# Attention's k: turned by VectorE in 32x32 squares and by DMAs through device memory, and the output product cut in two halves

## Chip, cores and metric

The kernel runs on one core of a Trainium2 chip, in fp32 throughout. The metric is the device time of one execution in microseconds (us), taken as the median of several runs. The engines are named as in the profile: PE is TensorE (PEld its weight loads), DVE is VectorE, ACT is ScalarE, POOL is GpSimd, SP is SyncE, which here only issues DMAs.

## The reference

The input x is 2 x 2048 x 256. Four residual blocks follow each other, each on a layer norm of x: a gated linear scan, a feed-forward layer with ternary weights, a higher-order linear attention (`hla`), and the same feed-forward layer again. The change lies in the attention:

```python
q = (x @ W_q).reshape(b, t, H, DK).transpose(1, 0, 2, 3)   # H = 16 heads, DK = DV = 64
k = (x @ W_k).reshape(b, t, H, DK).transpose(1, 0, 2, 3)
v = (x @ W_v).reshape(b, t, H, DV).transpose(1, 0, 2, 3)
def step(carry, qkv):
    S_K, C_QV, G = carry
    q_t, k_t, v_t = qkv
    k_C = einsum('bhk,bhkv->bhv', k_t, C_QV)
    G = G + k_t[..., :, None] * k_C[..., None, :]
    S_K = S_K + k_t[..., :, None] * k_t[..., None, :]
    C_QV = C_QV + q_t[..., :, None] * v_t[..., None, :]
    S_C = einsum('bhkj,bhjv->bhkv', S_K, C_QV)
    o_t = einsum('bhk,bhkv->bhv', q_t, S_C - G)
    return ((S_K, C_QV, G), o_t)
_, outs = scan(step, zeros, (q, k, v))
return outs.reshape(b, t, H * DV) @ W_o
```

## The kernel before

Three stages stand in program order: `front` (scan and first feed-forward layer), `attention`, and the second feed-forward layer. Within a stage PE, DVE, ACT and POOL run their instructions in the order in which the code issues them (`manual_schedule`); each engine works through its own queue in order and waits by semaphores for what it reads and for the buffers that it overwrites.

The attention works in 32 steps s (`NS`), one for each chunk of 128 tokens of each of the 2 sequences: step s is sequence s % 2, chunk n = s // 2. Even steps are called `first` in the code. The 1024 features of 16 heads are 8 pairs (`NPR`) of two heads, 128 features each; a chunk is processed as two halves of 64 tokens (`CH`). The projections q, k and v of two chunks, one for each sequence, are made together by seven products instead of eight (class `Seven`, its method `go`). They are spread over the steps: k of the next pair of steps is made in an even step, q and v in an odd one. `kN` holds k with tokens on the partitions. The operands q and k of the first product have to lie with features on the partitions (`qT`, `kT`); `qT` is made so at once, `kT` is turned from `kN`.

A step issues, in this order:

- `inter(s, "S", "uT")` (L838): q times the running sum S of k k^T, into `huT`;
- `products(s, "kT", "p1")` (L819): 64 small products of q and k into the two banks `hp`; DVE multiplies them by a causal mask into `p1` (L826);
- `outward(s - 2)` (L893): the output product of step s-2, 8 products of 128x256 into `hy`, which the trace shows as 16 matmuls; DVE adds `hy` to x (L898);
- `intra(s, "S", ..., "p1", "uT")` (L852) and `intra(s - 1, "M", ..., "p2", "oT")`: the masked part of this step and, one step late, of the second product; ACT and DVE copy the banks to `uT` and `oT`;
- parts of the projections, and between them `units(s)`: 8 transposes of u (`huN`, L805) which DVE copies to `uN` (L806);
- `update` (L874): S for step s+1 and M for step s, whose chunk sums DVE adds (L884);
- more of the projections, then `inter(s, "M", "oT")` and `products(s, "uT", "p2")` with its masks;
- the last product of k (even steps) or q (odd steps) and, in odd steps, the transposes of the next normalised x (`pt`, L199, copied by ACT, L202);
- `keys(s + 1)`: 8 transposes of k for the next step (`hkT`, L805) into two banks, which DVE copies to `kT` (L806).

In the last two steps parts of the first block of the next stage (`last.fill`) take the place of the projections. Before the loop, `keys(0)` and the projections of the first pair fill a start-up part. Each buffer named here is single (`bufs=1`), except `qT`, `kN`, `vN` and the sums with three. The PSUM has 8 banks in three rings: four "ps" (used by `hp`, `hy`, `hkT`, `huN`, `hS`, `hM`, `pt` and one bank of each projection), two "uT" and two "oT"; `bank` takes the next of its ring. The DMAs of the loads are issued at the start by SP and ACT; in the attention no DMA is issued before the output stores of its end.

In `front`, `ternary_sum` adds up the sizes of w1 on DVE (L225), `ternary_total` adds the 8 partial sums (L236), and `ternary_scale` sums over partitions by a product `pm` on PE (L242).

Of the kernel before, what the change touches and what calls it, by code (L numbers as in the profile page):

```python
# [17 lines left out]
FP = mybir.dt.float32  # L18
AF = mybir.ActivationFunctionType
ALU = mybir.AluOpType  # L20
AX = mybir.AxisListType

P = 128
B, T, D = 2, 2048, 256
# [4 lines left out]
NPR = H * DK // P  # L29
NCH = B * T // P  # L30
CPB = T // P
BC = 4
BT = BC * P
NBLK = T // BT
CH = 64
HF, HB, HD, HK = NF // 2, BT // 2, D // 2, H * DK // 2
LN_EPS = 1e-5
RMS_EPS = 1e-12
# [3 lines left out]
def kernel(  # L42
# [15 lines left out]
    nc = tc.nc  # L58
# [7 lines left out]
    def bank(shape, name, tag="ps"):  # L66

        ring = rings[tag]
        ring.append(ring.pop(0))
        return psum_pool.tile(shape, FP, tag=f"bank{ring[-1]}", bufs=1, name=name)  # L70
# [6 lines left out]
    x_sb = const.tile([P, NCH, D], FP, name="x_sb")  # L77
# [156 lines left out]
    def ternary_total(pool, part, name):  # L234
        tot = pool.tile([P, 1], FP, tag="tot", name=f"tot_{name}")
        nc.vector.tensor_reduce(tot, part, AX.X, ALU.add)  # L236
        return tot

    def ternary_scale(pool, w, tot, name):
        n = w.shape[1] * w.shape[2]  # L240
        pm = bank([P, 1], f"pm_{name}")
        nc.tensor.matmul(pm, lhsT=ones, rhs=tot, start=True, stop=True)  # L242
        hs = pool.tile([P, 1], FP, tag="hs", name=f"hs_{name}")
        nc.vector.tensor_scalar(hs, pm, 1.0 / (P * n), 1e-8, ALU.mult, ALU.max)
        nc.vector.tensor_scalar_mul(hs, hs, 0.5)
        nhs = pool.tile([P, 1], FP, tag="nhs", name=f"nhs_{name}")
        nc.vector.tensor_scalar_mul(nhs, hs, -1.0)
        return hs, nhs
# [281 lines left out]
    def front(scan_pool, ffn_pool, tern_pool, then, later):  # L530
        last = [{} for _ in range(B)]
# [35 lines left out]
        scales = {}  # L567

        def quarters_1():
            scales[1] = ternary_scale(tern_pool, w1, ternary_total(tern_pool, sum1, "w1"), "w1")  # L570
            tern(w1, scales[1], 0)
            tern(w1, scales[1], 1)

# [10 lines left out]
        s_(2)  # L584
        t_(1)
        q_(0, 1)
        sum1 = ternary_sum(tern_pool, w1, "w1", True)
        r_(2)
        q_(1, 0)
        s_(3)  # L590
# [99 lines left out]

    def attention(keep, pool, state, last):
        halves = [slice(0, CH), slice(CH, P)]

        def feats(h, p):
# [114 lines left out]
        def products(s, left, nm):  # L811


            b, n = steps[s]
            banks = [bank([P, NPR, CH], f"h{nm}{b}_{n}_{h}") for h in range(2)]
            for p in range(NPR):
                for c in range(2):
                    for h in range(2):
                        nc.tensor.matmul(  # L819
                            banks[h][halves[c], p, :], lhsT=d[s][left][halves[h], p, halves[c]],  # L820
                            rhs=d[s]["qT"][halves[h], p, halves[c]], start=True, stop=True,
                        )
            d[s][nm] = []
            for h in range(2):
                pm = pool.tile([P, NPR, CH], FP, tag=f"{nm}{h}", bufs=1, name=f"{nm}{b}_{n}_{h}")
                nc.vector.tensor_tensor(pm, banks[h], mask8, ALU.mult)  # L826
                d[s][nm].append(pm)

        def inter(s, sums, nm):

# [14 lines left out]
        def intra(s, sums, nat, pm, nm, evict):  # L845

            b, n = steps[s]
            banks = d[s][nm + "b"]
            for p in range(NPR):
                for c in range(2):  # L850
                    for h in range(2):
                        nc.tensor.matmul(  # L852
                            banks[c][halves[h ^ c], p, :], lhsT=d[s][nat][halves[c], feats(h, p)],
                            rhs=d[s][pm][h][halves[c], p, :],
                            start=(d[s][sums][c] is None and p == 0), stop=True,
                            skip_group_check=True,
                        )
            t = pool.tile([P, NPR, P], FP, tag=nm, bufs=1, name=f"{nm}{b}_{n}")
            evict(t[:, :, halves[0]], banks[0])  # L859
            for h in range(2):  # L860
                evict(t[halves[h], :, halves[1]], banks[1][halves[h ^ 1], :, :])
            d[s][nm] = t
# [23 lines left out]
                prev = t  # L886
            before[b, sums] = prev

        def outward(s):
            b, n = steps[s]  # L890
            py = bank([P, D], f"hy{b}_{n}")
            for p in range(NPR):
                nc.tensor.matmul(  # L893
                    py, lhsT=d[s]["oT"][:, p, :], rhs=wo[:, p, :],
                    start=(p == 0), stop=(p == NPR - 1),
                )
            xs = x_sb[:, b * CPB + n, :]
            nc.vector.tensor_tensor(xs, xs, py, ALU.add)  # L898

        def keys(s):  # L900
            kN = d[s]["kN"]
            turned(lambda p: kN[:, p * P : (p + 1) * P], s, "kT")

        def units(s):
            uT = d[s]["uT"]
# [12 lines left out]
        k.go(0, 5, 6)  # L918
        q.go(0, 5, 6)
        xn = norm_rows(norm_pool, pair(1), stats)  # L920
        k.go(7)
        q.go(7)
        k.go(3)
        q.go(3)
        k.go(4)
        q.go(4)
        v = Seven(0, "vN", "oT")
        v.go(2, 1)
        keys(0)
        v.go(0, 5, 6)  # L930
        update(0, "kN", "kN", "S")
        v.go(7, 3)
        for s in range(NS):
            first, n = s % 2 == 0, s // 2
            more = n + 1 < CPB
            inter(s, "S", "uT")
            products(s, "kT", "p1")
            if first and n + 2 < CPB:
                stats = norm_stats(norm_pool, pair(n + 2), bias=True)
            elif s == NS - 4:  # L940
                last.stats()
            elif s == NS - 2:
                last.second_stats()
            if s == 0:
                v.go(4)
                pairs[1] = norm_turned(norm_pool, pair(1), xn, bufs=1)
                pair_sums(1)
            if s % 2 == 1 and more:
                q, v = Seven(n + 1, "qT", "uT"), Seven(n + 1, "vN", "oT")
            if s == 1:  # L950
                q.go(2)
                v.go(2)
            if s >= 2:
                outward(s - 2)
                d[s - 2].clear()
            intra(s, "S", "kN", "p1", "uT", act)
            if s > 0:
                intra(s - 1, "M", "vN", "p2", "oT", dve)
            if not more:
                last.begin(first)  # L960
                fill = last.fill
                fill(2)
                units(s)
                fill(2)
            elif first:
                k = Seven(n + 1, "kN", "uT")
                k.go(2, 1)
                units(s)
                k.go(0, 5, 6)
            else:  # L970
                if s > 1:
                    q.go(2)
                    v.go(2)
                q.go(1)
                units(s)
                v.go(1)
                q.go(0, 5)
                v.go(0, 5)
                q.go(6)
                v.go(6)  # L980
            if first and n + 2 < CPB:
                xn = norm_rows(norm_pool, pair(n + 2), stats)
            elif s == NS - 4:
                last.rows()
            elif s == NS - 1:
                last.second_rows()
            if s + 1 < NS:
                update(s + 1, "kN", "kN", "S")
            update(s, "uN", "vN", "M")
            if not more:  # L990
                fill(2)
            elif first:
                k.go(7, 3)
            else:
                v.go(7)
                q.go(7)
                v.go(3, 4)
                q.go(3)
            inter(s, "M", "oT")
            products(s, "uT", "p2")  # L1000
            if not more:
                fill(1)
            elif first:
                k.go(4)
            else:
                q.go(4)
            if not first and n + 2 < CPB:
                pairs[n + 2] = norm_turned(norm_pool, pair(n + 2), xn, bufs=1)
                pair_sums(n + 2)
            elif s == NS - 3:  # L1010
                last.turned()
            if s + 1 < NS:
                keys(s + 1)
        last.out()
        outward(NS - 2)
        intra(NS - 1, "M", "vN", "p2", "oT", act)
        last.out()
        outward(NS - 1)

    pairs = {}  # L1020

# [83 lines left out]
    with tc.tile_pool(name="keep", bufs=3) as keep_pool:  # L1105
        with (
            tc.tile_pool(name="attn", bufs=1) as attn_pool,
            tc.tile_pool(name="state", bufs=1) as state_pool,
            tc.manual_schedule(engines=by_hand),
        ):  # L1110
            last = Last(keep_pool, attn_pool)
            attention(keep_pool, attn_pool, state_pool, last)

# [62 lines left out]
```

## Time and profile before

| | us |
|---|---|
| median of 3 runs (1275.59 to 1276.32) | 1275.65 |
| the profiled execution, its own time | 1276.43 |
| its span, from the first to the last instruction | 1274.2 |
| the attention's loop, from the first `hp` to the last transposes of k, about | 332 to 1054 |
| PE busy in 332 to 1054 (722.00) | 720.84 |
| DVE busy there | 418.61 |
| ACT busy there | 188.95 |

An even step in the middle took 20.2 us (560.28 to 580.49), an odd one some 24.6. The granted clock of PE is 1.00 throughout. The page puts the instructions in groups: line, engine, operation, output and inputs, shapes, count, then the busy time in us and the mean of one in ns, and behind a second bar how long the engine stood idle just before them and what ended that. The "chain that ended last" follows the program back from its end: at each piece to what released it, or to the piece before it on the same engine; in it pieces don't overlap, so its pieces can be added up, while the durations of the groups contain the latency of overlapping matmuls.

### The profile page before, as it was taken

What the parts mean: (1) busy time and instruction counts of PE and PEld (TensorE: products, weight loads), DVE (VectorE), ACT (ScalarE), POOL (GpSimd) and SP (SyncE); (2) the same over time, 40 slices, a digit from 0 to 9 for tenths busy, and PEclk for the clock granted to TensorE, in tenths of its full rate; (3) what the DMA queues carried; (4) which work ended last, traced back from release to release, by engine and by line L of the source; (5) the groups of instructions that cost most, each with busy time, mean ns of one, the idle gap of its engine ahead of it and who ended that gap; (6) DMA issues with size and microseconds to landing.
All of it is one profiled execution on the core that took longest, in us unless ns stands there. A gap on an engine that the chain in (4) does not pass through costs nothing.

```text
span 1274.2 us, 46893 instructions
## 1 busy us (share of the span) xinstructions
PE 1266.2 (99%) x21748; PEld 1031.6 (81%) x21748; DVE 748.7 (59%) x1375; ACT 435.3 (34%) x846; POOL 244.9 (19%) x427
## 2 busy tenths in 40 slices
PE   9999999999999999999999999999999999999998
PEld 6578877998677877877777778778778788999998
DVE  7965664655555555555555565565555665556654
ACT  4345554444322132222232222222222323444542
POOL 3742233331110110110110110110110120232221
PEclk9999999999999999999999999999999999999999
DMA  9100000000000000000000000000000000010000
GB/s 325 35 1 1 1 1 1 1 1 1 3 3 3 4 3 3 4 3 3 4 3 3 4 3 3 3 3 3 4 3 3 4 3 3 17 34 17 18 18 33
DMA packets 13042, 18.59 MB, mean 15 GB/s; under 512 B 784, under 2 KB 11792, under 8 KB 12848
## 3 DMA queue, kind: packets, MB, share of 16 engines
q1 hardware_dynamic: 12336, 15.21, 3.5%
q8 instruction: 170, 2.79, 0.9%
q0 software_dynamic: 80, 0.14, 0.1%
q10 hardware_dynamic: 432, 0.26, 0.1%
q14 instruction: 24, 0.20, 0.1%
HBM read 11.41 MB, written 4.19 MB: 12 GB/s over the span
## 4 chain that ended last, share of the span: by engine, by line
PE 98%; DMA 1%; DVE 1%; ACT 0%; issue 0%; POOL 0%; DVEq 0%; POOLq 0%
PE hy L893 9%; PE ox L473 9%; PE hx L382 9%; PE pq L269 6%; PE hkN_X L765 5%; PE hp L819 5%; PE hqT_X L760 5%; PE hvN_X L765 5%; PE oz L473 4%; PE hz L382 4%; PE huT L852 3%; PE hS L874 3%; PE huT L838 3%; PE hoT L838 3%; PE hM L874 2%; PE hoT L852 2%
## 5 line engine op out<-in xcount | busy, mean ns | idle before, releaser
L826 DVE TENSOR_TENSOR p<-hp,mask 128x512 f32<-128x512 f32 x128 | 82.4, 686 | 75.5 <-PE hp L819 75.5
L718 POOL TENSOR_TENSOR S<-xnT 128x128 f32<-128x128 f32 x32 | 14.6, 457 | 577.4 <-ACT xnT L202 559.7
L893 PE MATMUL hy<-wo,oT 128*128 128x256 f32 x512 | 119.2, 385 | 0.0
L893 PEld LDWEIGHTS hy<-wo,oT 128*128 128x128 f32 x512 | 94.6, 190 | 14.1 <-issue 0.5
L394 ACT ACTIVATE hT<-hT,b_sb 128x256 f32<-128x256 f32 x192 | 85.4, 500 | 33.9 <-DVE hT L426 32.4
L859 ACT COPY uT<-huT 128x512 f32<-128x512 f32 x32 | 18.8, 586 | 220.0 <-PE huT L852 220.0
L269 PE MATMUL pq<-xnT,wqkva 128*128 128x512 f32 (+1 forms) x216 | 85.0, 547 | 0.3 <-ACT xnT L213 0.3
L884 DVE TENSOR_TENSOR S<-S,hS 128x512 f32<-128x512 f32 x60 | 41.2, 687 | 71.7 <-PE hS L874 68.6
L269 PEld LDWEIGHTS pq<-xnT,wqkva 128*128 128x128 f32 x216 | 40.0, 190 | 37.5 <-issue 34.0
L185 ACT ACTIVATE xn<-x_sb,nb,rs 128x256 f32<-128x256 f32 x124 | 64.8, 592 | 16.1 <-POOL nb L171 16.1
L382 PE MATMUL hx<-xT,w 128*128 128x256 f32 x256 | 66.1, 381 | 0.0
L479 DVE TENSOR_TENSOR x_sb<-x_sb,ox 128x256 f32<-128x256 f32 x64 | 26.7, 417 | 63.7 <-PE ox L473 63.7
L806 DVE COPY uN<-huN 128x512 f32<-128x512 f32 x64 | 41.2, 685 | 22.7 <-PE huN L805 22.7
L382 PEld LDWEIGHTS hx<-xT,w 128*128 128x128 f32 x256 | 47.9, 190 | 6.4
L153 DVE BATCH_NORM_STATS2 st<-x_sb 128x6 f32<-128x256 f32 x128 | 51.3, 402 | 2.4 <-DMA x_sb<-in_x_dram 2.4
L359 POOL TENSOR_TENSOR xT<-xnT 128x256 f32<-128x256 f32 x15 | 10.9, 729 | 214.9 <-ACT xnT L215 214.9
L874 PEld LDWEIGHTS hS<-kN 64*64 64x64 f32 x1984 | 32.7, 134 | 23.8 <-DVE kN L770 10.6
L859 DVE COPY oT<-hoT 128x512 f32<-128x512 f32 x31 | 21.4, 691 | 50.7 <-PE hoT L852 50.7
L806 DVE COPY kT<-hkT 128x512 f32<-128x512 f32 x64 | 41.2, 686 | 16.6 <-PE hkT L805 16.6
L400 ACT COPY hT<-hx 128x512 f32<-128x512 f32 x32 | 18.8, 586 | 93.3 <-PE hx L382 93.3
L898 DVE TENSOR_TENSOR x_sb<-x_sb,hy 128x256 f32<-128x256 f32 x32 | 13.5, 421 | 52.8 <-PE hy L893 52.7
L465 DVE TENSOR_TENSOR hS<-hT 128x512 f32<-128x512 f32 x62 | 41.2, 685 | 5.6 <-ACT hT L394 5.6
(213 smaller groups left out, 2910.0 us busy)
## 6 DMA issues: line engine op xcount, KB each, us to landing
out_dram<-x_sb SPq DMA_DIRECT2D x16, 256.0 KB, 2.1
x_sb<-in_x_dram SPq DMA_DIRECT2D x7, 512.0 KB, 8.9
w<-in_w_t_dram SPq DMA_DIRECT2D x2, 512.0 KB, 8.9
w<-in_w_t_dram SPq DMA_DIRECT2D x1, 1024.0 KB, 11.1
wk<-in_w_k_dram SPq DMA_DIRECT2D x1, 1024.0 KB, 11.3
wq<-in_w_q_dram SPq DMA_DIRECT2D x1, 1024.0 KB, 12.2
wv<-in_w_v_dram SPq DMA_DIRECT2D x1, 1024.0 KB, 14.2
wo<-in_w_o_dram SPq DMA_DIRECT2D x1, 1024.0 KB, 15.7
```

The costliest lines, as they stand in the source:

```text
L185: nc.scalar.activation(xn[:, c, :], x_sb[:, g, :], AF.Identity, bias=nb[:, c : c + 1], scale=rs[:, c : c + 1],)
L269: nc.tensor.matmul(pq[:, :nt], lhsT=wqkva[:, d, col : col + P], rhs=xnT[:, d, :], start=(d == 0), stop=(d == ND - 1),)
L382: nc.tensor.matmul(at[a][:, j, :], lhsT=A[:, f * P : (f + 1) * P], rhs=Bm, start=(new and j == 0), stop=True, skip_group_check=True,)
L394: nc.scalar.activation(out, out if src is None else src[:, j, :], AF.Gelu, bias=b1_sb[:, f : f + 1])
L473: nc.tensor.matmul(banks[name][:, c, :], lhsT=A[f // 2][:, f % 2, c * P : (c + 1) * P], rhs=Bm[:, f, :], start=(new and c == 0 and f == 0) ...
L760: nc.tensor.matmul(to[:, j, :], lhsT=self.A[i][:, j * P : (j + 1) * P], rhs=self.B[i], start=(new and j == 0), stop=True, skip_group_check ...
L765: nc.tensor.matmul(to, lhsT=self.A[i], rhs=self.B[i], start=new, stop=True, skip_group_check=True)
L806: nc.vector.tensor_copy(t[:, 4 * g : 4 * g + 4, :], pt)
L826: nc.vector.tensor_tensor(pm, banks[h], mask8, ALU.mult)
L838: nc.tensor.matmul(banks[c][halves[h ^ c], p, :], lhsT=d[s][sums][c][halves[h], p, :], rhs=d[s]["qT"][halves[h], p, halves[c]], start=(p = ...
L874: nc.tensor.matmul(banks[c][halves[h], p, :], lhsT=d[s][left][halves[c], feats(h, p)], rhs=d[s][right][halves[c], feats(h, p)], start=True ...
L893: nc.tensor.matmul(py, lhsT=d[s]["oT"][:, p, :], rhs=wo[:, p, :], start=(p == 0), stop=(p == NPR - 1),)
```

## The change

`keys` no longer uses PE. Two steps ahead, at the end of step s, `keys_out(s + 2)` lets DVE turn the 32x32 squares of `kN` into `kS` (in the buffer of `uN`), and SP writes `kS` to device memory as `kD` (512 KB, three such buffers). In step s+1, after `intra`, `keys_in(s + 2)` (called there as `keys_in(s + 1)`) lets SP read `kD` by four DMAs, 32 partitions each, into `kR` (in the buffer of `p1`), where all features of a pair stand on the partitions but the pairs lie interleaved. Later in that step `keys` lets ACT copy `kR`, read at a step of 8 elements, into a contiguous `kT`. The output product is cut in two: `outward(s - 1, 0)`, its first four pairs, stands at the end of step s, `outward(s - 2, 1)`, the last four with the addition to x, in the old place. The masked products `p1` and `p2` become one tile each instead of two. At the start, product 7 and 3 of k are followed at once by `keys_out(0)` and `keys_in(0)`. In `front` the total of w1 is taken right behind its sum.

```diff
-            scales[1] = ternary_scale(tern_pool, w1, ternary_total(tern_pool, sum1, "w1"), "w1")
+            scales[1] = ternary_scale(tern_pool, w1, tot1, "w1")
...
-        sum1 = ternary_sum(tern_pool, w1, "w1", True)
+        tot1 = ternary_total(tern_pool, ternary_sum(tern_pool, w1, "w1", True), "w1")
...
-            d[s][nm] = []
+            d[s][nm] = pool.tile([P, 2, NPR, CH], FP, tag=nm, bufs=1, name=f"{nm}{b}_{n}")
             for h in range(2):
-                pm = pool.tile([P, NPR, CH], FP, tag=f"{nm}{h}", bufs=1, name=f"{nm}{b}_{n}_{h}")
-                nc.vector.tensor_tensor(pm, banks[h], mask8, ALU.mult)
-                d[s][nm].append(pm)
+                nc.vector.tensor_tensor(d[s][nm][:, h], banks[h], mask8, ALU.mult)
...
-        def outward(s):
+        def outward(s, half):
             b, n = steps[s]
-            py = bank([P, D], f"hy{b}_{n}")
-            for p in range(NPR):
+            if half == 0:
+                d[s]["y"] = bank([P, D], f"hy{b}_{n}")
+            py = d[s]["y"]
+            for p in range(half * NPR // 2, (half + 1) * NPR // 2):
                 nc.tensor.matmul(
                     py, lhsT=d[s]["oT"][:, p, :], rhs=wo[:, p, :],
                     start=(p == 0), stop=(p == NPR - 1),
                 )
-            xs = x_sb[:, b * CPB + n, :]
-            nc.vector.tensor_tensor(xs, xs, py, ALU.add)
+            if half == 1:
+                xs = x_sb[:, b * CPB + n, :]
+                nc.vector.tensor_tensor(xs, xs, py, ALU.add)
+                d[s].clear()
+
+        def keys_out(s):
+            b, n = steps[s]
+            kS = pool.tile([P, NQ, SQ, NPR], FP, tag="uN", bufs=1, name=f"kS{b}_{n}")
+            nc.vector.transpose(
+                kS.rearrange("p b j q -> p b q j"), d[s]["kN"].rearrange("t (q b i) -> t b q i", q=NPR, b=NQ)
+            )
+            kD = squares.tile([NQ, SQ, NQ, SQ * NPR], FP, tag="kD", bufs=3, name=f"kD{b}_{n}")
+            nc.sync.dma_start(out=kD.rearrange("a i b c -> (a i) b c"), in_=kS.rearrange("p b j q -> p b (j q)"))
+            d[s]["kD"] = kD
+
+        def keys_in(s):
+            b, n = steps[s]
+            kR = pool.tile([P, P, NPR], FP, tag="p1", bufs=1, name=f"kR{b}_{n}")
+            for b_ in range(NQ):
+                nc.sync.dma_start(
+                    out=kR[b_ * SQ : (b_ + 1) * SQ].rearrange("i (a j) q -> i a (j q)", a=NQ),
+                    in_=d[s]["kD"][:, :, b_, :].rearrange("a i c -> i a c"),
+                )
+            d[s]["kR"] = kR
 
         def keys(s):
-            kN = d[s]["kN"]
-            turned(lambda p: kN[:, p * P : (p + 1) * P], s, "kT")
+            b, n = steps[s]
+            kT = pool.tile([P, NPR, P], FP, tag="kT", bufs=1, name=f"kT{b}_{n}")
+            act(kT, d[s]["kR"].rearrange("p t q -> p q t"))
+            d[s]["kT"] = kT
...
-        k.go(7)
+        k.go(7, 3)
+        keys_out(0)
+        keys_in(0)
         q.go(7)
-        k.go(3)
-        q.go(3)
         k.go(4)
-        q.go(4)
+        q.go(3, 4)
         v = Seven(0, "vN", "oT")
         v.go(2, 1)
-        keys(0)
         v.go(0, 5, 6)
         update(0, "kN", "kN", "S")
         v.go(7, 3)
+        keys_out(1)
+        keys(0)
...
             if s >= 2:
-                outward(s - 2)
-                d[s - 2].clear()
+                outward(s - 2, 1)
             intra(s, "S", "kN", "p1", "uT", act)
             if s > 0:
                 intra(s - 1, "M", "vN", "p2", "oT", dve)
+            if s + 1 < NS:
+                keys_in(s + 1)
...
+            if s + 1 < NS:
+                keys(s + 1)
             inter(s, "M", "oT")
             products(s, "uT", "p2")
...
-            if s + 1 < NS:
-                keys(s + 1)
+            if s + 2 < NS:
+                keys_out(s + 2)
+            if s > 0:
+                outward(s - 1, 0)
         last.out()
-        outward(NS - 2)
+        outward(NS - 2, 1)
         intra(NS - 1, "M", "vN", "p2", "oT", act)
         last.out()
-        outward(NS - 1)
+        outward(NS - 1, 0)
+        outward(NS - 1, 1)
```

More of the change, by code (lines that the diff above doesn't have):

```diff
@@ L35 @@
 CH = 64
+SQ = 32
+NQ = P // SQ
 HF, HB, HD, HK = NF // 2, BT // 2, D // 2, H * DK // 2
@@ L683, in front, with attention @@
                 q_(u + 1, 1)
-    def attention(keep, pool, state, last):
+    def attention(keep, pool, state, squares, last):
         halves = [slice(0, CH), slice(CH, P)]
@@ L853, in intra @@
                             banks[c][halves[h ^ c], p, :], lhsT=d[s][nat][halves[c], feats(h, p)],
-                            rhs=d[s][pm][h][halves[c], p, :],
+                            rhs=d[s][pm][halves[c], h, p, :],
                             start=(d[s][sums][c] is None and p == 0), stop=True,
@@ L1108 @@
             tc.tile_pool(name="state", bufs=1) as state_pool,
+            tc.tile_pool(name="squares", bufs=2, space=bass.MemoryType.DRAM) as squares_pool,
             tc.manual_schedule(engines=by_hand),
@@ L1111 @@
             last = Last(keep_pool, attn_pool)
-            attention(keep_pool, attn_pool, state_pool, last)
+            attention(keep_pool, attn_pool, state_pool, squares_pool, last)
         with tc.tile_pool(name="ffn2", bufs=1) as ffn_pool, tc.manual_schedule(engines=by_hand):
```

## The prediction

> **What bounds the kernel now.** I read the shares of busy time first, then the chain that ended last, then one stretch of that chain in order of time, and VectorE's timeline over the same stretch.
>
> ```profile
> span 1274.2 us, 46893 instructions
> PE 1266.2 (99%) x21748; PEld 1031.6 (81%) x21748; DVE 748.7 (59%) x1375; ACT 435.3 (34%) x846; POOL 244.9 (19%) x427
> ...
> PE 98%; DMA 1%; DVE 1%; ACT 0%; issue 0%; POOL 0%; DVEq 0%; POOLq 0%
> ...
> L893 PE MATMUL hy<-wo,oT 128*128 128x256 f32 x512 | 119.2, 385 | 0.0
> ...
> L806 DVE COPY kT<-hkT 128x512 f32<-128x512 f32 x64 | 41.2, 686 | 16.6 <-PE hkT L805 16.6
> ```
>
> TensorE is the whole story: 98% of the chain is on it, and the list of TensorE's waits holds only 1.1 us for `pm_w`, 1.1 at one `hp`, 1.0 at the warm-up and some tenths. So what leaves TensorE's queue leaves the time, as long as nothing new makes it wait. A matmul's duration (385 ns for `hy`) is latency, since matmuls overlap; prices must come from the chain, whose pieces follow each other without overlap. The end of one even step and the start of the odd one:
>
> ```profile
> 577.63 0.93 PE hp L819 x64
> 578.56 1.06 PE hkN_X L765 x2
> 579.62 0.87 PE hkT L805 x8
> 580.49 1.09 PE huT L838 x64
> 581.58 0.93 PE hp L819 x64
> 582.52 3.65 PE hy L893 x16
> 586.17 1.09 PE huT L852 x64
> ```
>
> Here the eight transposes of k cost TensorE 0.87 us. A product after a switch between 128x128 and 64x64 weights costs more (`hkN_X` 1.06 against 0.86 elsewhere in the chain), some 0.2 us. So `hy` is 0.2 for the switch and 16 x 0.2156.
>
> ```profile
> 578.62 1.29 DVE L826 TENSOR_TENSOR p<-hp,mask 128x512 f32<-128x512 f32 x2 [0.83 <-PE hp L819]
> 580.09 1.29 DVE L806 COPY kT<-hkT 128x512 f32<-128x512 f32 x2 [0.19 <-PE hkT L805]
> 582.57 1.29 DVE L826 TENSOR_TENSOR p<-hp,mask 128x512 f32<-128x512 f32 x2 [1.19 <-PE hp L819]
> ```
>
> VectorE is free before each pair of masks. Between `hp` and the `huT` that reads the masked p1, TensorE is covered by `hy`.
>
> [...] No transpose by VectorE is in this trace. [...] the transpose writes and ScalarE reads at a step of 32 bytes. No row here shows that, so I carry a doubled duration as upper end.
>
> **The change part by part.**
>
> *Transposes leave TensorE.* The order of the instructions shows no `hkT` left; it was 8 in each of 32 steps. 32 x 0.87 = **27.8 us less** on the path. Its 64 copies on VectorE also go (1.29 us per step, beside other work).
>
> *`outward` in halves.* Same 8 products per step. The first half (8 x 0.2156 = 1.72 us) stands where `hkT` stood, behind a product with 128x128 weights, without a switch; the second keeps the place of `hy` with its switch, 1.92 us. 3.65 in sum, as before: **0**. What moves is cover. Between the end of k's last product and the next `huT` it grows from 0.87 to 1.72 us, good for ScalarE's copy of kN (0.59). Between `hp` and the reader of p1 it shrinks from 3.65 to 1.92. The masks end 582.57 + 1.29 - 582.52 = 1.34 us after `hy` began, so 0.58 us stay, less about 0.1 for the signal (in step 0 TensorE followed the mask by 0.08 us). Cost 0 while VectorE is free in time. The PSUM bank of `hy` is now held across two products; the next taker of that bank in the ring is `huN` or `hvN_Y`, over 3 us after `hy`'s addition can run: 0.
>
> *VectorE's squares* (`keys_out`, once per step). From 128x256 at 421 ns (L898) and 128x512 at 686 comes 1.04 ns per element, so 1024 elements take about **1.2 us** (estimate)[...]. They stand behind the p2 masks, which end at 579.91, and ahead of the next p1 masks. In the new order those start at 579.62 + 1.72 + 1.09 + 0.93 + 0.06 = 583.42. Room 3.5 us, and 0.5 beyond it before TensorE stalls: hidden at both ends. Behind the transpose wait only masks and later VectorE work, which had 1.29 us of copies there.
>
> *The transfers.* The DMA list gives issue to landing:
>
> ```profile
> out_dram<-x_sb SPq DMA_DIRECT2D x16, 256.0 KB, 2.1
> x_sb<-in_x_dram SPq DMA_DIRECT2D x7, 512.0 KB, 8.9
> ...
> x_sb<-in_x_dram SPq DMA_DIRECT2D x2, 128.0 KB, 2.7
> ```
>
> *The write* `kD` (SyncE, 512 KB, one issue). 2.1 us for 256 KB and 0.8 for 256 KB more at the 325 GB/s of the page's first slice: 2.9 us; no more than the 8.9 us that 512 KB took in the crowded load at the start. It is issued at a step's start and two wait for it: VectorE's `uN` copy (same buffer), some 8.3 us into the step, and the reads. At 8.9 us the copy would slip by half a us, but `hM` reads `uN` only at 11.7 (573.69 - 560.28, less the 1.73 us of `hy` moved away), so TensorE doesn't wait.
>
> *The reads* `kR` (four issues of 128 KB on SyncE). They wait for `intra` of p1 (same buffer), 5.0 us into the step: huT 1.09 + hp 0.93 + half 1.92 + huT 1.09. 2.7 us for one and 0.4 for each further: about 4 us, at most 8.9. Behind them on SyncE stands only the next `kD`, a half step later; output stores come after the last of both.
>
> *ScalarE's copy* of kT: 586 ns for 512 elements and 0.83 ns for each further (471 to 683 ns in the two sizes of L213): 1.0 us, 2.1 at the doubled rate. TensorE reads kT in the next step after `huT`, 20.4 us after this step's start for even steps (20.2 - 0.87 + 1.09), later for odd ones. Reads landed at 5.0 + 4 = 9, or 14 at worst, plus 2.1. Hidden with 4 us to spare at worst. ScalarE's queue: behind the copy stands kN's or qT's last copy, 3 us later, so even 2.1 us delays nothing; a late read would hold it, and with it the bank that `huT` needs.
>
> *Start.* The first round trip has no step before it. k's product 7 starts at 318.56 in the chain and product 3 now follows it directly; with 0.86 us each and VectorE's addition of 0.69, kN is done near 321.1, turned at 322.4, written at 325.4, read at 329.4, copied at 330.5. `hp` of step 0 comes at 331.4 (332.26 in the chain, less the 0.88 of `hkT` there). Bounds 0 and 4.3 us (at 8.9 for the reads); I take **0.5**. Once, at the end of step 0, there is neither `hkT` nor a half of `hy` to cover ScalarE's kN copy: 0.2 + 0.59 = **0.8 us**.
>
> *The earlier total of w1.* `pm_w` waited 1.1 us on TensorE because `tot_w` (154 ns) stood behind VectorE's statistics and scan. It now stands right behind its sum, 6 us ahead. **1.1 us less**, or 0 if a later wait takes it back.
>
> Sum against the profiled execution: its time is 1276.43 us (2.2 around the span of 1274.2). -27.8 - 1.1 + 0.8 + 0.5 = -27.6, so 1248.8. The median of the runs, 1275.65, lies 0.8 below: **1248.0 us**.
>
> **Rivals.**
>
> *TensorE waits for the p1 masks.* Against it: 0.5 us of slack. For it: the cover is halved, and transposes over 3.9 us would eat it[...]. Each 0.1 us over costs 3.1 us in 31 steps; a transpose of 4.3 us gives about +12, so 1260.
>
> *The round trip by way of memory is late, the case that ends slower.* If the reads land later than 14 us after their issue (5.0 + 14 + 1.0 against 20.4), every even step waits, and from about 16 us in 16 even steps the gain of 27.6 is gone. At 18 us: 16 x 3.6 = 58 us, so 1306. For it: a chain of five transfers with 1 KB runs into 32 partitions each, which the trace doesn't show. Against it: 11.1 to 15.7 us is what 1 MB took with other loads queued; here 512 KB run alone.
>
> *No gain*, where stalls of 0.9 us per step replace the transposes: it takes both lateness terms at odd sizes, so it is thin.
>
> **How the numbers follow.** The forecast holds with 0.83: 1247.5 (no start wait) to 1252.9 (start at 4.3, no gain at `pm_w`). Late masks or a small wait per step 0.09, 1252 to 1270. Round trip late 0.05, above 1278; no gain 0.03. I widen by 1.5 us below for gaps that the chain hides, and to 1257 above for 0.15 us per step: 1246 to 1257. A measurement of this kernel tells about 0.2% (2.6 us) from no change. Faster 0.91, same 0.03, slower 0.06.
>
> **What would show it.** Right: no `hkT`, TensorE still 98% of the chain, `hy` in pieces of 1.72 and 1.92, transposes near 1.2 us, no wait of TensorE on `kT` beyond step 0, `pm_w` without its 1.1. Wrong: idle time of TensorE in front of `hp` (`kT` from ScalarE) or of `huT` L852 (mask), or of VectorE's `uN` copy ended by a DMA.

## The result and the profile after

The changed kernel took **1253.0 us** (median of 4 runs, 1252.18 to 1253.3) against 1275.68 before in the same comparison: ratio 0.982, 95% interval 0.9803 to 0.9837. The time is 5.0 us above the forecast 1248.0. The profiled execution took 1252.95 us, its span 1251.2, so 23.0 less span than before where the steps of the prediction added up to 27.6. The 4.6 us between the two are what the experiments are about.

The page of the changed kernel, the lines that answer to those shown of before:

```profile
span 1251.2 us, 46884 instructions
...
PE 1240.6 (99%) x21492; PEld 1002.6 (80%) x21492; DVE 768.3 (61%) x1343; ACT 497.9 (40%) x878; POOL 244.3 (20%) x427
...
PE 97%; DMA 1%; DVE 0%; issue 0%; ACT 0%; SPq 0%; POOL 0%; ACTq 0%; DVEq 0%; POOLq 0%
...
L930 ACT COPY kT<-kR 128x1024 f32<-128x1024 f32 x32 | 66.2, 2069 | 1.7 <-DMA kR<-kD 1.7
...
L908 DVE STREAM_TRANSPOSE kS<-kN 128x1024 f32<-128x1024 f32 x32 | 65.3, 2039 | 0.0
...
kD<-kS SPq DMA_DIRECT2D x32, 512.0 KB, 3.0
kR<-kD SPq DMA_DIRECT2D x128, 128.0 KB, 3.1
```

TensorE lost 256 matmuls (21,748 to 21,492: the 8 `hkT` of 32 steps) and still carries the chain. VectorE and ScalarE pay 2.04 and 2.07 us per step. ScalarE waited for a read 1.7 us in all, in the start only. The same stretch of the chain of waits as shown of before, the end of an even step and the start of the odd one (start, duration, piece):

```profile
570.98 1.73 PE hy L895 x8
572.70 1.09 PE huT L838 x64
573.79 0.93 PE hp L821 x64
574.73 1.92 PE hy L895 x8
576.65 1.09 PE huT L852 x64
```

`hy` stands here in two pieces of 1.73 and 1.92, and nothing of `hkT` is left. VectorE's timeline beside it:

```profile
571.18 2.04 DVE L908 STREAM_TRANSPOSE kS<-kN 128x1024 f32<-128x1024 f32 x1
574.84 1.29 DVE L827 TENSOR_TENSOR p<-hp,mask 128x512 f32<-128x512 f32 x2 [1.62 <-issue]
```

The squares end at 573.22, 1.6 us before the masks; the masks end at 576.13, 0.52 us before `huT` L852 reads them. An undisturbed even step, counted from `hp` to the next `hp`, went from 20.10 to 19.23 us, an odd one from 26.86 to 25.99 or 26.00: 0.87 each. (From `huT` to `huT` the odd step of the kernel before took 26.87 as well, 580.49 to 607.36; the 24.6 given for it further above is wrong.)

So the loop earns exactly its 0.87 per step wherever nothing disturbs it. The list of TensorE's waits shows what disturbs it (us in total, times, longest):

```profile
PE hoT L852 <- issue: 1.3, 4, 0.4
PE huT L852 <- issue: 1.0, 3, 0.5
...
PE hqT_X L762 <- DVE qT L772: 0.9, 1, 0.9
...
PE hp L821 <- ACT kT L930: 0.4, 1, 0.4
```

Two rows are the start. The two upper rows are new: TensorE stopping *inside* a run of 64x64 products, with nothing shown to wait for. One of them in the chain, in an odd step:

```profile
894.88 1.92 PE hy L895 x8
896.80 1.09 PE huT L852 x64
897.89 0.23 PE hoT L852 x15
898.12 0.32 issue
898.44 0.93 PE hoT L852 x49
```

15 products of one run, 0.32 us of nothing, and then the other 49. To add these up I take from the trace the start of each step's first `hp` matmul, and for steps 2 to 29 the time beyond the undisturbed step (for step 29, 0.35 longer in nearly every kernel, beyond its own 27.21 before and 26.34 after). This **excess** is 2.2 us before and 6.5 after. With it the whole difference is placed; the forecast's terms are put where they belong (us, from the start of TensorE's warm-up, one profile of each kernel):

| stretch | forecast | measured |
|---|---|---|
| up to the first `hp` | -1.1 - 0.87 + 0.5 = -1.5 | 331.01 to 330.89: -0.12 |
| step 0 | -0.87 + 0.8 = -0.07 | 17.16 to 16.13: -1.02 |
| steps 1 to 30 and what follows the last `hp` | 30 x -0.87 = -26.1 | -21.84, of it +4.3 excess |
| sum | -27.6 | -23.0 |

### The profile page after: what moved, and what is told of

It reads as the page before. It is cut to its first block, busy times and chain, and to the rows that moved or that the text cites. A ratio compares the mean times of both kernels' runs of the same rounds, so it can differ in the third digit from the quotient of the medians.

```text
span 1251.2 us, 46884 instructions
## 1 busy us (share of the span) xinstructions
PE 1240.6 (99%) x21492; PEld 1002.6 (80%) x21492; DVE 768.3 (61%) x1343; ACT 497.9 (40%) x878; POOL 244.3 (20%) x427
## 3 DMA queue, kind: packets, MB, share of 16 engines
q8 instruction: 168, 2.75, 0.9%
## 4 chain that ended last, share of the span: by engine, by line
PE 97%; DMA 1%; DVE 0%; issue 0%; ACT 0%; SPq 0%; POOL 0%; ACTq 0%; DVEq 0%; POOLq 0%
PE hy L895 9%; PE ox L475 9%; PE hx L384 9%; PE pq L271 6%; PE hp L821 5%; PE hkN_X L767 5%; PE hqT_X L762 5%; PE oz L475 5%; PE hvN_X L767 5%; PE hz L384 4%; PE huT L852 3%; PE hoT L838 3%; PE hS L874 3%; PE huT L838 3%; PE hoT L852 3%; PE hM L874 2%
## 5 line engine op out<-in xcount | busy, mean ns | idle before, releaser
L895 PE MATMUL hy<-wo,oT 128*128 128x256 f32 x512 | 123.9, 385 | 0.0
L930 ACT COPY kT<-kR 128x1024 f32<-128x1024 f32 x32 | 66.2, 2069 | 1.7 <-DMA kR<-kD 1.7
L908 DVE STREAM_TRANSPOSE kS<-kN 128x1024 f32<-128x1024 f32 x32 | 65.3, 2039 | 0.0
```

Of the source, the lines that this page charges most:

```text
L895: nc.tensor.matmul(py, lhsT=d[s]["oT"][:, p, :], rhs=wo[:, p, :], start=(p == 0), stop=(p == NPR - 1),)
L908: nc.vector.transpose(kS.rearrange("p b j q -> p b q j"), d[s]["kN"].rearrange("t (q b i) -> t b q i", q=NPR, b=NQ))
L930: act(kT, d[s]["kR"].rearrange("p t q -> p q t"))
```

## The experiments

**The theories.** Where do 4.3 us of short stalls come from? *Crowding* (T1 in the expectations): the second half of `hy` is only 1.92 us long, so the 64x64 runs stand closer together behind `hp`. *Traffic*: the new transfers get in the way of another one. The records of the trace suggest which: beside the data, the page lists a queue of the kind "instruction", q8, with 168 packets of 2.75 MB, 16 KB each. The kernel before has 170 packets there, so 512 matmuls and weight loads fewer (42,984 against 43,496) went with two packets fewer. From these counts I take the queue to carry TensorE's instructions, at 64 bytes each and 256 per transfer (an estimate: 2.75 MB over 42,984). A 64x64 run uses up 128 in 0.93 us. Each of the 12 stalls over 0.12 us inside a run of 64x64 products in the attention of the changed kernel ends 1.24 to 1.57 us after the end of such an instruction transfer. And in 7 of the 12 (3.5 us together) that transfer started within 0.01 us of the end of a packet of the write `kD` while no other of its packets was under way: in 5 it was the write's last packet, in steps 27 and 29 one and two more followed behind the instruction transfer. The other five are in `hM` of steps 20, 22 and 24, far from the write, and in steps 9 and 17; in step 9 the instruction transfer ran among the write's packets and took 1.70 us, where without data transfers (e3, below) none took over 1.45. Hence *theory W*: the write holds back the instruction transfer, and TensorE stops until its instructions have come; *theory R*: the reads `kR` do. A third possibility is that the forecast had overlooked a cost of the squares or of the copy.

All runs, with the median of the kernel before in their comparison (1275.68 for the change and e1 to e4, 1275.95 for e5 to e8, 1276.19 for e9 to e11):

| kernel | us, median (range) | ratio to before, 95% interval | excess, us |
|---|---|---|---|
| the change | 1253.0 (1252.18 to 1253.3) | 0.982 (0.9803 to 0.9837) | 6.5 |
| e1 two to six | 1249.37 (1249.09 to 1249.58) | 0.9795 (0.9781 to 0.9808) | 1.8 |
| e2 traffic alone | 1285.21 (1284.45 to 1285.9) | 1.0074 (1.0061 to 1.0088) | |
| e3 no DMA | 1247.87 (1247.82 to 1247.93) | 0.9783 (0.977 to 0.9797) | 1.1 |
| e4 rows | 1247.66 (1247.05 to 1247.93) | 0.9781 (0.9768 to 0.9794) | 2.2 |
| e5 total alone | 1274.65 (1273.67 to 1276.45) | 0.9989 (0.9981 to 0.9997) | |
| e6 hy whole | 1263.6 (1263.39 to 1263.86) | 0.9901 (0.9888 to 0.9915) | |
| e7 no write | 1247.75 (1246.9 to 1248.01) | 0.9776 (0.9762 to 0.9789) | 1.1 |
| e8 no read | 1252.72 (1251.99 to 1252.94) | 0.9815 (0.9801 to 0.9828) | 5.5 |
| e9 rows, two to six | 1247.86 (1246.85 to 1248.49) | 0.9777 (0.9764 to 0.9791) | 1.7 |
| e10 rows, early | 1246.89 (1246.24 to 1247.52) | 0.9769 (0.9756 to 0.9782) | 1.9 |
| e11 all three | 1247.8 (1247.35 to 1248.31) | 0.9778 (0.9764 to 0.9791) | 2.1 |

### e1: two products of `hy` first, six later

```diff
-            for p in range(half * NPR // 2, (half + 1) * NPR // 2):
+            for p in (range(2, NPR) if half else range(2)):
```

> The output product is cut 2 to 6 instead of 4 to 4, nothing else. Against the changed kernel (1253.0 us). Theory 1 (TensorE runs out of instructions where two dense runs of 64x64 products follow each other too closely[...]): 2.8 us of hy stand between them instead of 1.9, so the stalls inside L852 and L874, 4.8 us in 12 places in the changed kernel, fall to 2 us or less and the time to about 1250. Theory 2 (the DMA traffic of k delays the instruction transfers): same traffic, so 1253 and 4 to 5 us of stalls.

1249.37 us, 3.6 less than the change. The excess falls from 6.5 to 1.8; 0.8 of that is lost again in step 30, the last but one, where 0.86 us of `hy` no longer cover a copy by ScalarE (`huT` waits 0.5 for `hT`). This is what crowding was expected to give, and not what traffic was (1253). But two things moved with the split. `huT` L852 comes 0.86 us later behind `hp`; and the write, which stays with VectorE's work, now starts 0.9 us later after `hp`, so that in the four steps of the table further below the instruction transfer began (0.44 to 1.06 us after `hp`) before the write's first packet (0.88 to 1.35). So e1 doesn't say which of the two removes the stalls, and not what makes them.

### e2: the traffic put onto the kernel before

The squares, the write and the four reads are added to the kernel before, whose `hkT` and whole `hy` stay; what is read isn't used.

```diff
+            if s + 1 < NS:
+                keys_in(s + 1)
...
                 keys(s + 1)
+            if s + 2 < NS:
+                keys_out(s + 2)
```

> The kernel before, with its transposes on TensorE and hy whole, and beside it the squares on VectorE and the DMAs of k, whose result nobody reads; TensorE's instructions are those of the kernel before. Against 1275.7 us. Theory 1 (crowded 64x64 runs): 1275 to 1277, the stalls in 64x64 runs as before, about 1.4 us in 2 places. Theory 2 (traffic): stalls of 4 to 5 us in some 12 places, near the reads kR, and 1279 to 1280.

1285.21 us, but not by the loop: its undisturbed steps are those of before to 0.01 us. The 9.5 us lie in step 0 (26.75 us instead of 17.16), where `p1` shares its buffer with `kR` and its masks had to await the first reads (`huT` L852 waited 6.5 us for the mask, once). That wait comes from how I built this kernel. In its loop the write's packets run from 2.8 to 4.2 us after the start of `hp` (medians), where 3.65 us of `hy` follow `hp`. Traffic alone, at that place and with that cover, costs next to nothing: one stall of 0.5 us, in `hoT` of step 7, and there too the instruction transfer began within 0.01 us of the write's end. It doesn't acquit the traffic of the changed kernel, where it stands elsewhere.

### e3: no transfers

`kT` is copied from `kS` straight away, so it holds squares that were never moved between partitions, and k in the first product is not the right one. The copy moves to the step's start, since `kS` has a single buffer.

```diff
-            kD = squares.tile([NQ, SQ, NQ, SQ * NPR], FP, tag="kD", bufs=3, name=f"kD{b}_{n}")
-            nc.sync.dma_start(out=kD.rearrange("a i b c -> (a i) b c"), in_=kS.rearrange("p b j q -> p b (j q)"))
-            d[s]["kD"] = kD
+            d[s]["kR"] = kS.rearrange("p b j q -> p (b j) q")
...
```

> The changed kernel without the DMAs of k: the squares are turned by VectorE and copied by ScalarE, but not moved between partitions, which is left out; ScalarE's copy comes right behind the products of the step before. Against 1253.0 us. Theory 1 (crowded 64x64 runs): stalls stay near 4 to 5 us, and only the start's wait for the round trip, 0.4 us, goes: about 1252.5. Theory 2 (traffic): stalls fall to 1.4 us or less, and the time to about 1249.

1247.87 us, excess 1.1. With the split of four to four, and so with the crowding, the stalls are gone with the transfers (two are left, in step 0 and in `hM`): traffic it is, and the crowding only takes away the slack.

### e4: the squares in contiguous rows

The squares are laid out by pair, so that VectorE writes and ScalarE reads 32 neighbouring elements at a time instead of one in every 32 bytes. Nothing is left out, and the transfers are as large as before.

```diff
-            kS = pool.tile([P, NQ, SQ, NPR], FP, tag="uN", bufs=1, name=f"kS{b}_{n}")
+            kS = pool.tile([P, NQ, NPR, SQ], FP, tag="uN", bufs=1, name=f"kS{b}_{n}")
             nc.vector.transpose(
-                kS.rearrange("p b j q -> p b q j"), d[s]["kN"].rearrange("t (q b i) -> t b q i", q=NPR, b=NQ)
+                kS, d[s]["kN"].rearrange("t (q b i) -> t b q i", q=NPR, b=NQ)
...
-            act(kT, d[s]["kR"].rearrange("p t q -> p q t"))
+            act(kT.rearrange("p q (a j) -> p q a j", a=NQ), d[s]["kR"].rearrange("p a q j -> p q a j"))
```

> The changed kernel with the squares laid out by pair, so that VectorE's transpose writes, and ScalarE's copy reads, 32 elements in a row instead of single ones at a step of 32 bytes; same sizes and same DMA runs of 1 KB. If the step of 32 bytes is what doubled them: transpose 1.2 us instead of 2.04, copy 1.05 instead of 2.07; the time changes only at the start, where TensorE waited 0.9 us for an addition behind the first transpose and 0.4 for kT: about 1251.7. If the doubled price is one of fp32 or of these operations: 2.0 us each and 1253.

1247.66 us. The groups of this kernel:

```profile
L930 ACT COPY kT<-kR 128x1024 f32<-128x1024 f32 x32 | 33.3, 1040 | 1.4 <-DMA kR<-kD 1.4
...
L908 DVE STREAM_TRANSPOSE kS<-kN 128x1024 f32<-128x1024 f32 x32 | 39.5, 1235 | 0.0
```

Both instructions nearly halve (2069 to 1040 ns, 2039 to 1235). Its span is 5.5 us below that of the change: 1.3 in the start (`hqT_X` waits 0.2 instead of 0.9, and no `hp` waits for `kT`), 4.3 of excess, 0.2 back in step 0. The loop had cover for the slow squares, so why do the stalls go? Because the write is issued 0.8 us sooner: its packets run from -0.80 to 0.72 us around the start of `hp` in even steps instead of 0.00 to 1.59 (odd: -0.34 to 1.22 instead of 0.47 to 2.56; medians), and are mostly over when the instruction transfer is due, which in the four steps of the table below begins 0.62 to 1.08 us after `hp`. I had expected 1251.7, a gain at the start alone. Of the 4 stalls that are left, 2 still lie behind an instruction transfer that began at the write's end.

### e7 and e8: the write or the reads

In e7 the write is left out from step 2 on, and the reads fetch the squares of the first two steps again and again. In e8 the reads are left out, and `kT` is copied from `kS` as in e3. In both, k in the first product is not the right one.

```diff
+        held = {}
...
+            if s > 1:
+                d[s]["kD"] = held[s % 2]
+                return
             kD = squares.tile([NQ, SQ, NQ, SQ * NPR], FP, tag="kD", bufs=3, name=f"kD{b}_{n}")
...
+            held[s] = kD
```

> The changed kernel with the write kD left out from step 2 on: every later read takes the squares of steps 0 and 1 again, so the same reads with other steps' k. Theory W (the write holds up an instruction transfer for TensorE that falls into its 1.6 to 2.1 us, and L852, coming soon after, runs dry): stalls fall to 1 us or less, about 1248.5. Theory R (the reads do it): stalls stay at 4 to 5 us, 1253.

```diff
+            d[s]["kR"] = kS.rearrange("p b j q -> p (b j) q")
...
-            kR = pool.tile([P, P, NPR], FP, tag="p1", bufs=1, name=f"kR{b}_{n}")
-            for b_ in range(NQ):
-                nc.sync.dma_start(
...
+            return
...
```

> The changed kernel with the reads kR left out: the write stays, ScalarE copies the squares from VectorE's buffer behind the products of the step before, so the move between partitions is left out. Theory W (the write): stalls of 4 to 5 us stay, 1252 to 1253. Theory R (the reads): stalls of 1 us or less, about 1248, as without both.

Without the write 1247.75 us and an excess of 1.1; without the reads 1252.72, an excess of 5.5, and 10 of 12 stalls behind an instruction transfer that began within 0.01 us of the end of a packet of the write, 8 of them of its last. The intervals of the two don't overlap. And the code of e8 differs from that of e3 in the write alone: 1252.72 against 1247.87. W stands, R falls. The step shown above with its stall, now in the chain of e7:

```profile
891.62 1.93 PE hy L895 x8
893.55 1.09 PE huT L852 x64
894.64 0.93 PE hoT L852 x64
```

The run of 64 is in one piece. The transfers' records, for four steps with a stall (us after the start of the step's first `hp` matmul; taken from the trace):

| step | write's packets, the change | instruction transfer, the change | the same one in e7 | in e3 |
|---|---|---|---|---|
| 3 | 0.47 to 2.33 | 2.33 to 3.21 | 0.90 to 2.10 | 1.19 to 2.13 |
| 14 | 0.00 to 1.92 | 1.92 to 2.86 | 0.53 to 1.47 | 0.52 to 1.39 |
| 16 | 0.00 to 1.93 | 1.93 to 2.86 | 1.08 to 2.00 | 0.41 to 1.50 |
| 25 | 0.47 to 2.41 | 2.42 to 3.34 | 1.01 to 2.13 | 1.02 to 2.44 |

Where the write is missing, the instruction transfer comes 0.85 to 1.5 us sooner. That TensorE stands in a stall for want of these instructions is inferred from these times and from the 1.24 to 1.57 us between a transfer's end and TensorE's going on; no view shows which instructions it holds.

### e5: the early total of w1, alone on the kernel before

```diff
-            scales[1] = ternary_scale(tern_pool, w1, ternary_total(tern_pool, sum1, "w1"), "w1")
+            scales[1] = ternary_scale(tern_pool, w1, tot1, "w1")
...
-        sum1 = ternary_sum(tern_pool, w1, "w1", True)
+        tot1 = ternary_total(tern_pool, ternary_sum(tern_pool, w1, "w1", True), "w1")
```

> The kernel before with the early total of w1 alone. If nothing later takes the 1.1 us of pm_w back: 1274.6 against 1275.7. If the front's other waits absorb it: 1275.7.

1274.65 us, ratio 0.9989, interval 0.9981 to 0.9997: 1.4 us less by the ratio, 0.4 to 2.4 by its interval. `pm_w` has left the list of TensorE's waits, and in the changed kernel k's first product began at 309.26 us after the start of the warm-up instead of 310.35: 1.09 less. One profile doesn't settle the size: over the eleven kernels with the early total this start lies at 308.56 to 309.82, so 0.5 to 1.8 us sooner.

### e6: `hy` whole, in its old place

```diff
-            if half == 0:
+            if half == 1:
                 d[s]["y"] = bank([P, D], f"hy{b}_{n}")
...
+            for p in (range(NPR) if half else ()):
```

> The changed kernel with the output product whole in its old place and nothing where the first half stood. If the half is needed as cover for ScalarE's last copy (0.2 + 0.59 us before huT L838 may take its bank; the transposes of x cover 0.44 of it in odd steps): some 0.8 us in 16 even steps and 0.35 in 15 odd ones, 18 us, less the 4 us of stalls that the longer distance of the 64x64 runs takes away: about 1267. If huT doesn't wait for that copy: about 1249, and the halves bring nothing.

1263.6 us, 10.6 above the change. The list of TensorE's waits:

```profile
PE huT L838 <- ACT kN L798: 9.5, 14, 0.7
PE huT L838 <- ACT qT L798: 3.3, 14, 0.2
```

Without half of `hy` at the step's end, `huT` waits for ScalarE to empty its bank, 0.7 us in even steps and 0.2 in odd ones, and the steps take 19.97 and 26.30. Cutting `hy` costs TensorE nothing (1.73 and 1.92 us in the change, 3.65 whole) and is what turns the removed transposes into time. No 64x64 run stalls over 0.12 us in this kernel. As in e1, two things moved: 3.65 us of `hy` stand behind `hp`, and the write starts some 1.45 us after it, when in the four steps of the table the instruction transfer had begun (0.80 to 1.20).

### e9, e10, e11: the remedies together

e9 is e4 with the split of e1. e10 is e4 with the squares ahead of the p2 masks, e11 all three.

```diff
+            if s + 2 < NS:
+                keys_out(s + 2)
             products(s, "uT", "p2")
...
-            if s + 2 < NS:
-                keys_out(s + 2)
```

> Squares laid out in contiguous runs (as in the rows layout) and hy split two products to six, so that the 64x64 product after the second part comes 0.43 us later behind each hp. Theory W (the write of kD holds up TensorE's instruction transfers, and what is left of it is 1.6 us of stalls): both remedies act on the same stalls, so they do not add to 1247.66 - 6.3; stalls fall from 1.6 to some 0.3 us and the time is about 1246.3 (1245.5 to 1247.2). If the rows layout had gained by something else than these stalls, the gains would add: 1253.0 - 5.3 - 3.6 = 1244.

> Rows layout, and the squares and their write are put ahead of the p2 masks of the same step instead of behind them. VectorE has then 1.24 us of squares in front of the p2 masks. Theory W: the write's packets end well before hp, so the instruction transfer that follows hp is free: stalls 0.3 to 0.5 us, about 1246.5. Rival: the masks of p2, 1.2 us late, are waited for: the squares run while hp runs (0.93 us), so 0.3 us of lateness must show as a wait of hM on p2 if there is no slack there; then 31 x up to 0.3 = up to 9 us more, 1257.

> All three: rows layout, two products to six, squares ahead of the p2 masks. Theory W: no more than e9 or e10 alone, about 1246 (stalls 0 to 0.3 us); the floor is the sum of the moved work, 1253.0 less the 4.8 us of stalls less the 1.5 us of the start = 1246.7, within 0.7. Should one of the remedies have a cost of its own (p2 masks late), it shows here as in e10.

The remedies don't add up, as theory W has it: all three lie with e4 and e3, their intervals overlap, and the excess stays at 1.7 to 2.1, where before had 2.2. e9 also parts what e1 moved together: its write runs again where that of the change does (from 0.06 us after `hp` in even steps, 0.53 in odd ones; medians), and in the four steps of the table the instruction transfer is as late as there (1.92 to 2.51), but `huT` L852 comes 3.83 us after `hp` instead of 2.97, and none of these steps stalls. So the longer cover is enough alone, and e4 and e10 show that an earlier write is too. I had expected stalls of 0 to 0.5 us inside runs; they add up to 1.7 in e9, 0.7 in e10 and 1.7 in e11 (1.6 in e4). None of those in e9, e10 and e11 lies behind an instruction transfer that began at the end of a packet of the write; what makes them stays open. In e10 the write's packets are over 0.5 to 1.7 us before `hp` in the steps of the table, and the write can't have made the two stalls that remain: for one, in `hoT`, the instruction transfer began 3.4 us after the write's end, the other is in `hM`, far from any write. e9 and e11 also lost 0.9 and 0.7 us in step 30, 20.10 and 19.92 us against 19.25; 0.6 and 0.4 of that are a stall inside `hp`, so the missing cover of e1 costs less here. The masks of p2, 1.2 us later in e10, are not waited for. e10 has the lowest median, 1246.89; it is better than the change (0.9769 against 0.982, intervals apart), but not told apart from e4.

## Why the prediction was right, and where it was short

**Transposes, 27.8 us:** right. Each undisturbed step lost 0.87.

**`hy` in halves, 0:** right in the sizes (1.72 and 1.92 forecast, 1.73 and 1.92 measured) and in both covers: no wait for kN's copy in the loop, and 0.52 us of slack at the masks where 0.58 less 0.1 was forecast. The rival of late masks did not happen, although the squares, at 2.04 us, came near the doubled 1.2.

**Squares and copy:** the base values 1.2 and 1.0 us were those of contiguous rows (1.235 and 1.040 in e4); the layout of the change took 2.04 and 2.07, near the doubled ones (twice 1.2, and 2.1). No row of the profile before showed an access at a step of 32 bytes, so the doubling was my assumption; measured against e4, that step cost a factor of 1.65 on VectorE's write and of 2.0 on ScalarE's read.

**Round trip:** right, and the slower rival with it excluded. The write took 2.85 us in the chain (2.9 forecast). The reads took 4.6 in the start, from the first issue at 325.09 to the landing at 329.66 (about 4 forecast). In the loop `kT`'s copy began at 565.47 for an `hp` at 573.79.

**Start, +0.5:** too small. Without the 0.87 of `hkT` and the 1.09 of `pm_w` the stretch up to the first `hp` should have shrunk by 1.96 and shrank by 0.12: 1.84 instead of 0.5. The chain there:

```profile
320.02 2.04 DVE kS L908
...
322.22 2.85 DMA kD<-kS
...
329.81 2.08 ACT kT L930
...
331.94 1.16 PE hp L821 x64
```

The forecast followed only this path, with 1.2 and 1.0 for its two instructions; with 2.04 and 2.08 it came 0.4 us late. And it left out what stood behind the squares on VectorE in the start: q's addition, for which TensorE's `hqT_X` waited 0.9. These are idle times; from start to start of the products the two waits cost 0.7 and 1.05 us. In e4, whose squares and copy have the prices of the forecast, the same stretch costs 0.3. The question what is queued behind a new instruction was asked for the loop and not for the start.

**End of step 0, +0.8:** did not occur. `huT` began at 347.38, right behind k's last product, while ScalarE copied that product's bank from 347.42 to 348.01. It could go on beside the copy, because in the first chunk of a sequence there is no earlier sum yet: `inter` then skips its first bank (`continue` in the code) and issues 32 products, which the trace has in steps 0 and 1, instead of 64. They all go to the second bank, and k's last product lies in the first. In e6, at the same place of an ordinary even step, `huT` waited 0.7 us. I hadn't followed the banks through.

**Total of w1, -1.1:** right (1.09 between the two profiles, within the 0.5 to 1.8 of e5's section).

**The step that failed** is the 0 for the transfers' neighbours. I asked who waits for the write and what stands behind it on SyncE, and not which other transfers go at that time: the instructions of TensorE. In the same way the cover behind `hp` was cut from 3.65 to 1.92 us with a look at the masks alone, which had 0.5 us to spare; a late instruction transfer had less. That is 4.3 of the 4.6 us. The other 0.3 or so are the start (+1.3) and step 0 (-1.0), which nearly cancel. A sign stood in the profile before, the 1.1 us at one `hp` in the list of waits, which the prediction names and passes over:

```profile
796.57 0.93 PE hp L819 x60
797.50 1.06 issue
798.56 0.33 PE hp L819 x4
```

It is a stall of the same kind: TensorE goes on 1.39 us after the end of an instruction transfer (795.97 to 797.17). No data transfer ran there; what made it is not known.

**The range** held with some luck. The terms themselves gave 1247.5 to 1252.9, and 1253.0 lies just outside. The "gaps that the chain hides" lay on the other side, and for the 0.15 us per step added above no cause was named; that the stalls came to 4.3 over 30 steps, 0.14 each, is chance.

## What to carry to other kernels

When a change puts transfers into a stretch that had none, look at the instruction queue in the DMA list too: TensorE used 128 instructions in a 64x64 run of 0.93 us here, where one transfer brought 256 (estimate from the counts above), and a store of 512 KB issued just ahead of such a run put that transfer off by 0.85 to 1.5 us. Two remedies worked: issue the store earlier (e4, e10), or let some longer instructions stand between it and the dense run (e9). An "issue" piece inside a run of equal products is the sign to look for, before the change too. And ask of every new instruction what stands behind it in the start-up part too, where nothing covers it.

## What the runs showed of the hardware that I had not expected

- The change's write of 512 KB, 128 packets of 4 KB, delayed a 16-KB instruction transfer until its last packet (4 steps in the table, 0.85 to 1.5 us later than in e7 and e3) or, in two more of the 12 stalls, the last but one or two, although in the step shown its packets took only 67% of the time of the 16 DMA engines between its start and its end (1.31 of 1.95 us).
- TensorE went on 1.24 to 1.57 us after the end of the instruction transfer before it in the 12 stalls of the change.
- Stepping by 32 bytes, in the change against e4, raised VectorE's transpose of 128x1024 elements from 1.235 to 2.04 us, and ScalarE's copy from 1.04 to 2.07.
- Reads in runs of 1 KB landed in 3.1 us for 128 KB, about as fast as the plain loads of that size (2.7).
